# Gathers in buffers of two groups, layer 2 one step later, transposes moved up, and last node parts placed by hand in a graph layer

## The chip, the core and the metric

One Trainium2 chip, one core of it. The metric is the device time of one execution in microseconds (us); it is the median of three runs. The profile is of one further execution of the same program on the chip.

## What is computed

A message-passing layer on 12,500 nodes with 64 features and 200,000 edges sorted by target, then a residual and a layer norm. In short:

```python
nodes = x[edges].reshape(E, 128)                     # x[src] beside x[dst], gathered per edge
gates = ssp(edge_attr @ We1 + be1) @ We2 + be2       # ssp(v) = softplus(v) - log 2
gates = gates * (1 - sigmoid(5 * (dist - 3.5)))
h     = ssp(nodes @ Wn1 + bn1) @ Wn2 + bn2
msum  = zeros_like(x).at[dst].add(h * gates)         # sums over the edges of each target node
y     = x + (x + (ssp(msum @ Ws1 + bs1) @ Ws2 + bs2))
out   = (y - mean(y)) / sqrt(var(y) + 1e-5)
```

All of it is in float32.

## The kernel before, in words

**Groups and steps.** The edges go in NG = 391 groups of 512 (two halves of 256, four chunks of 128 lanes, K = 4). The main loop runs over steps `i` from -3 to 388; in one step different groups are in different stages, so a step has the work of one group altogether. The order on each engine is the order in which the code calls things (`tc.manual_schedule()`); waits between engines are put in by the framework.

**The start.** The part of `x[dst] @ Wn1` is first made once per node as a table in DRAM ("the table phase", L497 to L519): 14 pieces, each of 7 matmuls (L501), a copy by ACT (L503), one by DVE (L504), a store, and a memset of the buffer that becomes `sums` (L506).

**Gathers.** `gather(g)` (L173) fetches `x[src]` for a group: four indirect DMAs issued by POOL (L183), one per chunk, into an `xg` buffer. 12 groups out of 391 (`by_rows`) have three, and their last chunk comes by single rows on SP's queue (`fetch`, L198). There are AHEAD + 5 = 25 `xg` buffers, one per group. Six groups are gathered at once, one more after each of the 14 table pieces (its gather waits for a one-column memset on DVE, L178, which stands behind that piece), and in step `i` the group `i + 19`. A gather into a used buffer waits for the last reader of the group that had it, 25 groups earlier: the scatter matmul of L292.

**One step `i`, before.** On PE: `layer2_edge(i-1)` (L266 bias, L269); `layer1_edge(i+1)` (L233 bias, L235) into a new `z` tile (two of them, in PSUM); node-block matmuls, if any are due; `layer1_node(i+1)` (L241); `scatter(i-3)` (L292) into the free end of the same `z` tile; `transposes(i+3)` (L224) into a `tx` tile (two); `layer2_node(i-1)` (L275) into the `gh` tile (two). On ACT: `exps` and `logs` of group `i+1` (L252, L255), then `xcopy(i+3)` (L229, `tx` to SBUF). On DVE: `hcut` and `message` of `i-1` (L284, L288), `window(i-3)` (L308, adds the scatter's result to `sums`), `softplus(i+1)` (L260), `onehot(i+5)` (L216). SP loads edge features and table rows some steps ahead (L204, L211).

`second`, `third` and `ahead` say which groups are in layer 2, scatter and transposes in a step. Near the end (from `ends = last - CATCH_UP` = 373) the order in a step changes and the lags shrink, so that the last groups are not strung out.

**Node blocks.** 25 blocks of up to 512 nodes are finished as soon as all their edges are summed: `node_block` returns 11 parts (fetch, hidden L327, logs, center, ssp, layer2 L358, add, square, variance, root, scale and store), which `BLOCK_STEPS` spreads over the steps that follow. The last block is done after the loop (L620 to L647).

Of the kernel before, what the change touches and what calls it, by code (L numbers as in the profile page):

```python
# [42 lines left out]
F32 = mybir.dt.float32  # L43
# [13 lines left out]
P = 128  # L57
D = 64
HE = 256
GE = 2 * HE  # L60
W = 42
# [1 line left out]
PIECES = 3  # L63
NB = 512
K = 4
AHEAD = 20
LOADS = 5
SPREADS = 5
CATCH_UP = 17
PREPARE = 5  # L70

BLOCK_STEPS = ((2, 3, 4, 4, 6, 7, 8, 9, 10, 14), (2, 3, 3, 4, 5, 6, 7, 8, 9, 10), (1, 1, 1, 2, 3, 3, 4, 4, 4, 4))
ROWS = 4
CUTOFF = 5.0
EPS = 1e-5
# [28 lines left out]
def gnn_resnorm_kernel(ctx: ExitStack, tc: tile.TileContext, a: dict, out: bass.AP, E: int):  # L104
# [67 lines left out]

    def gather(g, after=False):  # L173

        xg = loads.tile([P, K, P], F32, name="xg", bufs=AHEAD + 5)
        xgs[g] = xg
        if after:
            nc.vector.memset(xg[:, 0, :1], 0.0)  # L178
        for k in range(K - (g in by_rows)):
            if padding(g, k):  # L180
                nc.vector.memset(xg[:, k, :D], 0.0)
                continue
            nc.gpsimd.indirect_dma_start(  # L183
                out=xg[:, k, :D], out_offset=None, in_=x,
                in_offset=bass.IndirectOffsetOnAxis(ap=src_i[:, g, k : k + 1], axis=0))
# [70 lines left out]

    def softplus(g, part=every):
        if part.start == 0:
            ss[g] = work.tile([P, 3, 2, P], F32, name="s", bufs=3)
        nc.vector.scalar_tensor_tensor(ss[g].rearrange("p i t e -> p (i t e)")[:, part], us[g][:, part], BIG,  # L260
                                       z_of(g)[:, part], OP.min, OP.max)

    def layer2_edge(g):
        gh = gh_tile()
        v = gh.rearrange("p (i t h d) -> p i t h d", i=2, t=2, h=2)
        nc.tensor.matmul(gh, ones3[:, :P], row3.rearrange("q i k d -> q (i k d)"), start=True, stop=False,  # L266
                         skip_group_check=True)
        for t in range(2):
            nc.tensor.matmul(v[:, 0, t], ss[g][:, 0, t, :], we2, start=False, stop=False, skip_group_check=True)  # L269
        ghs[g] = gh.rearrange("p (i k d) -> p i k d", i=2, k=K)  # L270
# [127 lines left out]
    with tc.manual_schedule():  # L398
# [4 lines left out]
        with tc.tile_pool(name="prep", bufs=1) as prep:  # L403
# [15 lines left out]
            nc.sync.dma_start(dist, a["dist_l"])  # L419
            dst_i = rel.bitcast(I32)  # L420
            nc.sync.dma_start(dst_i.rearrange("p g k -> p (g k)"), a["dst_l"])
            FREE = AHEAD - 2 * PARTS
            for g in range(FREE):
                gather(g)

            nc.vector.memset(one, 1.0)
            nc.vector.memset(half, 0.5)
# [68 lines left out]
            for i in range(PARTS):  # L496
                for c in range(i * CP, (i + 1) * CP, CP // 2):  # L497
                    m = CP // 2
                    ps = z_tile().rearrange("p b (k f) -> p (b k) f", k=K)
                    for k in range(m):  # L500
                        nc.tensor.matmul(ps[:, k, :], xT[:, c + k, :], wnb, start=True, stop=True)  # L501
                    tb = prep.tile([P, m, 2 * D], F32, name="tb", bufs=6)
                    nc.scalar.copy(tb[:, :K, :], ps[:, :K, :])  # L503
                    nc.vector.tensor_copy(tb[:, K:, :], ps[:, K:m, :])  # L504
                    nc.sync.dma_start(by_node[:, c : c + m], tb)
                    nc.vector.memset(sums[:, c * P : WIDE if c + m == NCH else (c + m) * P], 0.0)  # L506
                    gather(FREE + c // m, after=True)
                if i == 1:
                    nc.vector.tensor_copy(base_i, base_b[:1])
                    for k in range(2):  # L510
                        nc.vector.tensor_copy(be3[:, k, :], rows[:, 0, :])
                    for k in range(K):
                        nc.vector.tensor_copy(row3[:, :, k, :], rows[:, 1:3, :])
                        nc.vector.tensor_copy(rs3[:, k, :], rows[:, 3, :])
                if i == 2:
                    nc.vector.tensor_copy(rel, dst_i)
                    for t in range(2):
                        r = rel[:, :, 2 * t : 2 * t + 2]
                        nc.vector.tensor_sub(r, r, base_b[:, :NH].rearrange("p (g h) -> p g h", h=2))  # L519


        with tc.tile_pool(name="finish", bufs=1) as finish:
# [5 lines left out]
            def lagging(i, lag, steps):  # L528

                lag -= sum(i > step for step in steps)  # L530
                return [g for g in range(i - lag, i - lag + 1 + (i in steps)) if g >= 0]

            for i in range(-3, NG):
                second[i] = lagging(i, 1, (ends + 5,))
                third[i] = lagging(i, 3, (ends - 2, ends + 8))
                ahead[i] = [i + 3] if i < ends else [i + 2] if i == ends + 1 else [i + 1] if i > ends + 2 else []
            parts, begun, complete = {}, None, 0

            def at(f, g, *more):
                if 0 <= g < NG:  # L540
                    f(g, *more)
# [5 lines left out]
            for i in range(-3, last - 1):  # L547
# [1 line left out]
                early = [part for part in now if part.tensor]  # L549
                at(load, i + LOADS)  # L550
                fetch(i)
                if i > 0:
                    at(gather, i + AHEAD - 1)
                if i < ends:
                    for g in second[i]:
                        layer2_edge(g)
                    if i >= -1:
                        zs[i + 1] = z_tile()
                        layer1_edge(i + 1)
                        for part in early:  # L560
                            part.tensor(tx_tile())
                    if i >= -1:
                        layer1_node(i + 1)
                    for n, g in enumerate(third[i]):
                        scatter(g, zs[i + 1][:, 1, HE + 2 * W * n : HE + 2 * W * (n + 1)])
                    at(exps, i + 1)
                    at(logs, i + 1)
                    for g in ahead[i]:
                        transposes(g)
                        xcopy(g)  # L570
                    for g in second[i]:
                        layer2_node(g)
                    for g in second[i]:
                        hcut(g)
                        message(g)
# [34 lines left out]
                    begun.pop(0).others()  # L610
                if blocks and complete >= blocks[0][1]:
                    steps = next(steps for steps in BLOCK_STEPS if i + steps[-1] < last - 1)
                    for n, part in zip(steps, begun, strict=True):
                        parts.setdefault(i + n, []).append(part)
                    blocks.pop(0)
                    begun = None
            assert len(blocks) == 1 and begun and not parts
# [8 lines left out]
            for some in (edge, node):  # L626
                exps(last, some)
                logs(last, some)
            for g in range(last - 2, last + 1):
                window_bases(g)  # L630
            layer2(last - 1)
# [5 lines left out]
            scatter(last - 1, tx_tile()[:, : 2 * W])  # L637
            softplus(last, node)
            window(last - 2)
            layer2_node(last)  # L640
            window(last - 1)
            hcut(last)
            message(last)
            scatter(last, tx_tile()[:, : 2 * W])
            window(last)
            for part in begun:
                node_part(part)  # L647

# [146 lines left out]
```

## Time and profile before

| what | value |
|---|---|
| median of three runs (2535.73 to 2542.47) | 2539.01 us |
| the profiled execution, own time | 2535.25 us |
| its span, first to last instruction | 2533.4 us |
| granted TensorE clock, mean | 0.866 |
| busy: PE, PE weight loads | 2139.0 us, 1735.4 us |
| busy: POOL, DVE, ACT | 1469.2 us, 1085.8 us, 920.1 us |
| gathers on POOL (L183) | 1551, 0.947 us each |
| exponentials (L252) | 392, 0.809 us each |

How to read it: busy times are of one engine each, and engines work beside each other, so they don't add up. "Idle before, released by" in a timeline row names whose signal came last by the profile before an instruction could start. PE's rows are pipelined, and their ends are modelled. A timeline row has the start in us from the span's start, the duration in us, the engine, the source line, the operation, the output tile with the input tiles, and in brackets the idle time before it.

### The profile page before, as it was taken

What the parts mean: (1) busy time and instruction counts of PE and PEld (TensorE: products, weight loads), DVE (VectorE), ACT (ScalarE), POOL (GpSimd) and SP (SyncE); (2) the same over time, 40 slices, a digit from 0 to 9 for tenths busy, and PEclk for the clock granted to TensorE, in tenths of its full rate; (3) what the DMA queues carried; (4) which work ended last, traced back from release to release, by engine and by line L of the source; (5) the groups of instructions that cost most, each with busy time, mean ns of one, the idle gap of its engine ahead of it and who ended that gap; (6) DMA issues with size and microseconds to landing.
All of it is one profiled execution on the core that took longest, in us unless ns stands there. A gap on an engine that the chain in (4) does not pass through costs nothing. (4 is left out here: it accounts for less than half of the span.)

```text
span 2533.4 us, 41076 instructions
## 1 busy us (share of the span) xinstructions
PE 2139.0 (84%) x11373; PEld 1735.4 (69%) x11373; DVE 1085.8 (43%) x2745; ACT 920.1 (36%) x1317; POOL 1469.2 (58%) x1555
## 2 busy tenths in 40 slices
PE   4569888988988888888879987988898889888897
PEld 3457676777767767667767766766777667766775
DVE  3224434444444444444444444444444444444553
ACT  1123333333333333333333433333434333333442
POOL 6655666666666666656666655566666666666400
PEclk9998889788888888888997888888888888899895
DMA  7312222222222222222222222222222222222210
GB/s 194 90 45 52 51 50 53 51 51 53 51 55 50 53 52 55 53 52 57 51 55 56 50 53 53 52 57 52 57 54 53 56 54 57 55 61 55 54 48 8
DMA packets 170982, 143.07 MB, mean 56 GB/s; under 512 B 46475, under 2 KB 142915, under 8 KB 170746
## 3 DMA queue, kind: packets, MB, share of 16 engines
q1 hardware_dynamic: 119746, 87.95, 12.0%
q0 software_dynamic: 49632, 50.92, 11.2%
q8 instruction: 93, 1.52, 0.3%
q10 hardware_dynamic: 1368, 1.51, 0.2%
q14 instruction: 143, 1.17, 0.1%
HBM read 130.57 MB, written 9.63 MB: 55 GB/s over the span
## 5 line engine op out<-in xcount | busy, mean ns | idle before, releaser
L183 POOL DMA_INDIRECT xg<-in_x,src_i x1551 | 1469.0, 947 | 919.4 <-issue 361.1
L252 ACT ACTIVATE u<-z 128x768 f32<-128x768 f32 x392 | 317.0, 809 | 1435.7 <-PE z L241 469.1
L284 DVE TENSOR_TENSOR h<-gh,cut 128x256 f32<-128x256 f32 x391 | 165.9, 424 | 1162.9 <-PE z L241 369.9
L241 PE MATMUL z<-xT,wns 106*128 106x256 f32 x1564 | 497.2, 448 | 7.1 <-issue 3.2
L275 PE MATMUL gh<-consts,s 128*128 128x64 f32 x3128 | 428.9, 284 | 7.0 <-issue 6.9
L269 PE MATMUL gh<-consts,s 128*128 128x128 f32 x1564 | 310.5, 326 | 141.7 <-issue 124.1
L275 PEld LDWEIGHTS gh<-consts,s 128*128 128x128 f32 x3128 | 423.6, 210 | 4.8 <-issue 4.8
L241 PEld LDWEIGHTS z<-xT,wns 106*128 106x128 f32 x1564 | 353.1, 228 | 78.7 <-issue 8.5
L269 PEld LDWEIGHTS gh<-consts,s 128*128 128x128 f32 x1564 | 229.0, 211 | 248.7 <-issue 222.7
L260 DVE SCALAR_TENSOR_TENSOR s<-u,z 128x768 f32<-128x768 f32 x392 | 372.7, 951 | 47.6 <-issue 26.2
L255 ACT ACTIVATE u<-u,one 128x768 f32<-128x768 f32 x392 | 365.9, 933 | 12.7
L224 PE MATMUL tx<-consts,xg 128*106 128x128 f32 x1552 | 278.4, 307 | 62.8 <-ACT u L255 29.4
L235 PE MATMUL z<-eT,consts 128*128 128x256 f32 x782 | 314.7, 489 | 0.0
L292 PEld LDWEIGHTS z<-xg,msg 128*128 128x128 f32 x1484 | 272.0, 227 | 47.5 <-issue 16.1
L292 PE MATMUL z<-xg,msg 128*128 128x84 f32 x1484 | 257.0, 298 | 21.1 <-issue 20.7
L224 PEld LDWEIGHTS tx<-consts,xg 128*106 128x106 f32 x1552 | 209.9, 160 | 86.6 <-issue 38.2
L229 ACT COPY xT<-tx 106x512 f32<-106x512 f32 x391 | 221.4, 566 | 35.9 <-PE tx L224 18.5
L308 DVE TENSOR_TENSOR sums<-sums,z 64x42 f32 x742 | 145.8, 197 | 129.1 <-issue 113.9
L288 DVE TENSOR_TENSOR msg<-gh,h 128x256 f32<-128x256 f32 x391 | 165.9, 424 | 13.4
L235 PEld LDWEIGHTS z<-eT,consts 128*128 128x128 f32 x782 | 131.9, 212 | 54.9 <-issue 16.1
L266 PE MATMUL gh<-row,ones 3*128 3x512 bf16 x391 | 156.9, 401 | 3.3 <-issue 2.5
L216 DVE TENSOR_TENSOR xg<-consts,rel 128x168 f32<-128x168 f32 x391 | 135.9, 348 | 0.2
(100 smaller groups left out, 635.7 us busy)
## 6 DMA issues: line engine op xcount, KB each, us to landing
eT<-in_eT SPq DMA_DIRECT2D x391, 128.0 KB
xg<-in_x,src_i POOLq DMA_INDIRECT x1551
xr<-in_x SPq DMA_DIRECT2D x1536, 0.2 KB
wns<-table SPq DMA_DIRECT2D x782, 21.0 KB
table<-tb SPq DMA_DIRECT2D x14, 448.0 KB
sums<-in_xT SPq DMA_DIRECT2D x7, 455.0 KB
y<-in_x SPq DMA_DIRECT2D x24, 128.0 KB
out<-y SPq DMA_DIRECT2D x24, 128.0 KB
```

What stands on the lines that cost most here:

```text
L183: nc.gpsimd.indirect_dma_start(out=xg[:, k, :D], out_offset=None, in_=x, in_offset=bass.IndirectOffsetOnAxis(ap=src_i[:, g, k : k + 1], ax ...
L224: nc.tensor.transpose(tx[:, k, :], row, ident)
L229: nc.scalar.copy(xT, xTs[g])
L235: nc.tensor.matmul(zs[g][:, 0, :HE], we1.rearrange("a h d -> a (h d)"), eTs[g], start=False, stop=True, skip_group_check=True)
L241: nc.tensor.matmul(zn, wns[:, g % REST, h, :], xTs[g][:, h], start=True, stop=True, skip_group_check=True)
L252: nc.scalar.activation(us[g][:, part], z_of(g)[:, part], AF.Exp)
L255: nc.scalar.activation(us[g][:, part], us[g][:, part], AF.Ln, bias=one)
L260: nc.vector.scalar_tensor_tensor(ss[g].rearrange("p i t e -> p (i t e)")[:, part], us[g][:, part], BIG, z_of(g)[:, part], OP.min, OP.max)
L269: nc.tensor.matmul(v[:, 0, t], ss[g][:, 0, t, :], we2, start=False, stop=False, skip_group_check=True)
L275: nc.tensor.matmul(ghs[g][:, 1, 2 * t + h, :], ss[g][:, 1 + h, t, :], wn2, start=False, stop=h == 1 and t == 1, skip_group_check=True)
L284: nc.vector.tensor_mul(hs[g], ghs[g][:, 1], cut[:, g, :].to_broadcast([P, K, D]))
L292: nc.tensor.matmul(sc, msgs[g][:, 2 * t : 2 * t + 2, :].rearrange("p h f -> p (h f)"), xgs[g][:, 2 * t : 2 * t + 2, D:DW], start=t == 0, s ...
```

## The change

- `xg` buffers hold two groups: one buffer `[P, 2, K, P]` for groups `2p` and `2p+1`, (AHEAD + BEHIND) // 2 = 11 of them, that is 22 groups in place of 25.
- Gathers of two groups are issued in every second step (`i` and even): groups `i + 16` and `i + 17`, the first with the DVE memset while `i < 6`.
- In the table phase seven groups are gathered at once and nine more at pieces 0, 1, 3, 5, 6, 8, 10, 11 and 13, so 16 groups and not 20.
- Layer 2 stands two steps behind (`i-2`), the scatter four (`i-4`); there are four `s` buffers in place of three. On PE a step is now: layer 2 (edge and node together), transposes, layer 1 edge, scatter, layer 1 node.
- The end begins 10 groups before the last and not 17, with new steps at which the lags shrink; the parts of the last but one block from the square on, and the last block's first, are placed by hand after the loop.

```diff
-AHEAD = 20
+AHEAD = 16
-CATCH_UP = 17
+CATCH_UP = 10
+FREE = 7
+BEHIND = 6
-BLOCK_STEPS = ((2, 3, 4, 4, 6, 7, 8, 9, 10, 14), (2, 3, 3, 4, 5, 6, 7, 8, 9, 10), (1, 1, 1, 2, 3, 3, 4, 4, 4, 4))
+BLOCK_STEPS = ((2, 3, 4, 4, 6, 7, 8, 9, 10, 14), (2, 3, 3, 4, 5, 6, 7, 8, 9, 10), (1, 2, 1, 2, 3))
...
     def gather(g, after=False):
-        xg = loads.tile([P, K, P], F32, name="xg", bufs=AHEAD + 5)
-        xgs[g] = xg
+        if g % 2 == 0:
+            pair = loads.tile([P, 2, K, P], F32, name="xg", bufs=(AHEAD + BEHIND) // 2)
+            xgs[g], xgs[g + 1] = pair[:, 0], pair[:, 1]
+        xg = xgs[g]
...
-            ss[g] = work.tile([P, 3, 2, P], F32, name="s", bufs=3)
+            ss[g] = work.tile([P, 3, 2, P], F32, name="s", bufs=4)
...
-            FREE = AHEAD - 2 * PARTS
-            for g in range(FREE):
-                gather(g)
+            waiting = {}
+            for g in range(AHEAD):
+                if g < FREE:
+                    gather(g)
+                else:
+                    waiting.setdefault(min(5 * (g - FREE) // 3, 2 * PARTS - 1), []).append(g)
...
-                    gather(FREE + c // m, after=True)
+                    for g in waiting.get(c // m, []):
+                        gather(g, after=True)
...
-                second[i] = lagging(i, 1, (ends + 5,))
-                third[i] = lagging(i, 3, (ends - 2, ends + 8))
+                second[i] = lagging(i, 2, (ends - 3, ends + 3))
+                third[i] = lagging(i, 4, (ends - 4, ends - 2, ends + 5))
...
-                if i > 0:
-                    at(gather, i + AHEAD - 1)
+                if i >= 0 and i % 2 == 0:
+                    at(gather, i + AHEAD, i < BEHIND)
+                    at(gather, i + AHEAD + 1)
                 if i < ends:
                     for g in second[i]:
-                        layer2_edge(g)
+                        layer2(g)
+                    for g in ahead[i]:
+                        transposes(g)
+                        xcopy(g)
                     if i >= -1:
                         zs[i + 1] = z_tile()
                         layer1_edge(i + 1)
                         for part in early:
                             part.tensor(tx_tile())
+                    for n, g in enumerate(third[i]):
+                        scatter(g, zs[i + 1][:, 1, HE + 2 * W * n : HE + 2 * W * (n + 1)])
                     if i >= -1:
                         layer1_node(i + 1)
-                    for n, g in enumerate(third[i]):
-                        scatter(g, zs[i + 1][:, 1, HE + 2 * W * n : HE + 2 * W * (n + 1)])
                     at(exps, i + 1)
                     at(logs, i + 1)
-                    for g in ahead[i]:
-                        transposes(g)
-                        xcopy(g)
-                    for g in second[i]:
-                        layer2_node(g)
...
-                    for n, part in zip(steps, begun, strict=True):
+                    for n, part in zip(steps, begun):
                         parts.setdefault(i + n, []).append(part)
+                    rest = begun[len(steps) :]
...
+            square, variance, root, scale, store = (part.others for part in rest)
+            square()
...
             window(last - 2)
+            variance()
+            root()
             layer2_node(last)
...
             window(last)
+            hidden, clamp = begun.pop(0)
+            hidden(gh_tile())
+            scale()
+            clamp()
+            store()
```

## The prediction

> **What bounds the kernel now.** I read the page first (PE 84% busy, POOL 58%, ACT 36%, DVE 43%: no engine is full), then the table of waits (ACT's L252, DVE's L284 and POOL's L183 all wait for PE, in turn for many different PE lines), then the timeline of all engines in an undisturbed stretch:
>
> ```profile
> 1202.15 0.94 POOL L183 DMA_INDIRECT xg<-in_x,src_i  x1 [1.46 <-PE tx L224]
> ...
> 1206.47 0.39 PE L266 MATMUL gh<-row,ones 3*128 3x512 bf16 x1
> 1206.53 0.81 ACT L252 ACTIVATE u<-z 128x768 f32<-128x768 f32 x1 [1.51 <-PE gh L275]
> ...
> 1206.76 0.42 DVE L284 TENSOR_TENSOR h<-gh,cut 128x256 f32<-128x256 f32 x1 [1.70 <-PE gh L275]
> 1206.77 0.94 POOL L183 DMA_INDIRECT xg<-in_x,src_i  x1 [1.18 <-PE gh L275]
> ...
> 1210.51 1.06 POOL L183 DMA_INDIRECT xg<-in_x,src_i  x1 [0.30 <-issue]
> 1210.82 0.39 PE L266 MATMUL gh<-row,ones 3*128 3x512 bf16 x1
> ...
> 1212.61 0.81 ACT L252 ACTIVATE u<-z 128x768 f32<-128x768 f32 x1 [3.83 <-PE z L233]
> ...
> 1212.84 0.42 DVE L284 TENSOR_TENSOR h<-gh,cut 128x256 f32<-128x256 f32 x1 [2.09 <-PE z L235]
> 1212.85 0.94 POOL L183 DMA_INDIRECT xg<-in_x,src_i  x1 [1.28 <-PE z L235]
> ```
>
> See that ACT, DVE and POOL, which wait for three different matmuls (L241, L275, L292), wake within 0.24 us of each other, 2.1 to 2.3 us after the last of a group's gathers was issued (1210.51). PE's own records come 4.35 us apart (1206.47 to 1210.82); the wakes are 6.08 us apart. The step that begins at 1202.15 has three gathers (its fourth chunk is one of the 12 by single rows) and lasts 4.62 us. So a step is as long as its gathers: while they run, news that PE has finished something is held back. POOL waits each step because its buffer is freed by PE's scatter, so the loop is POOL, PE's news, POOL. Over the trace I counted 340 cycles of four gathers, median 6.06 us.
>
> Two other places bear this out: a run of eight gathers (POOL), and, after the last gather (2387.93), ACT's rows of L252, which are then 4.5 us apart:
>
> ```profile
> 345.48 0.94 POOL L183 DMA_INDIRECT xg<-in_x,src_i  x1 [2.82 <-PE z L241]
> ...
> 354.22 0.94 POOL L183 DMA_INDIRECT xg<-in_x,src_i  x1 [0.30 <-issue]
> 357.21 0.95 POOL L183 DMA_INDIRECT xg<-in_x,src_i  x1 [2.04 <-PE z L292]
> ```
>
> ```profile
> 2427.21 0.81 ACT L252 ACTIVATE u<-z 128x768 f32<-128x768 f32 x1 [1.22 <-PE z L241]
> 2431.72 0.81 ACT L252 ACTIVATE u<-z 128x768 f32<-128x768 f32 x1 [1.22 <-PE z L241]
> ```
>
> The start shows the same on a larger scale: 32 gathers in a row (105.22 to 143.90) leave ACT waiting from 118.5 to 144.05 for all but a copy, and POOL resumes at 161.93:
>
> ```profile
> 116.67 0.81 ACT L252 ACTIVATE u<-z 128x768 f32<-128x768 f32 x1 [3.96 <-PE z L233]
> 144.05 0.81 ACT L252 ACTIVATE u<-z 128x768 f32<-128x768 f32 x1 [18.32 <-remote]
> ```
>
> **Budget of before**, from POOL's rows. POOL's first loop wait (group 25) ends at 161.93; its last (group 390) at 2385.43, 365 cycles later. 365 x 6.06 = 2211.9; the 12 short ones take 6.06 - 4.62 = 1.44 less each, 17.3; the remaining 2385.43 - 161.93 - 2211.9 + 17.3 = 28.9 is cycles lengthened by node blocks. From 2385.43 to the end are 148.0. Sum 2533.4, the span.
>
> **The change, part by part.**
>
> *The loop.* A gather of an even group now waits once for DVE's memset or for the scatter of a group 11 pairs earlier, and eight gathers (seven with a short group) follow without a wait: 365 cycles become 184 (first pairs waited for: 22/23; last 390). What does one cost? By the run of eight, 357.21 - 345.48 = 11.73; the other clean ones in the trace took 11.90, 12.14 and 12.22. Against 2 x 6.06 = 12.12, the lower end is what saving one of two restarts gives (four more gathers cost 11.73 - 6.06 = 5.67, 1.42 each). I take 11.85: the two low ones are nearer, because the high ones start amid node-block work. PE has 2 x 4.35 = 8.70 to do in it, and about 0.44 of node blocks (0.74 for L358 and the like, in some steps), so spare 2.7. 184 x 11.85 = 2180.4.
>
> For this to hold, PE must do two groups with the news of one wake. That is where the lag of two goes: layer 2 of group i-2 and i-1 can follow from softplus results that DVE made after one wake, and `z`, `gh` and `tx` have two buffers each, so PE can go two steps beyond what was reported. The exponential of the second step waits for its layer 1 as before; its news comes with the next wake.
>
> *The other moves of the order cost nothing while that holds:* the scatter stood between L241 and L252's release only in the free end of `z` (0.57 us, inside the held time); `xcopy` (0.56) now goes ahead of the exponential on ACT, inside ACT's 3.8-us idle time before L252 (1212.61); without that cover it is 0.56 a step. `onehot` of an even group now waits for eight gathers, but they were issued 11 steps earlier. SP's queue keeps its order: loads, fetches and table rows move past nothing. The counts of PE, ACT and DVE instructions stay; a fourth `s` buffer only takes a wait away. The memset is 0.06 us, in three steps only.
>
> *The start.* The table phase now stands behind 64 gathers and not 68 (17 groups were gathered by 105.22). 3.4 + 64 x 1.42 = 94.3, and some 3 us of gaps: the last piece at 97 where before it was about 107; 9.6 us on (softplus of group 0, as in before, 109.75 to 119.4) the first pair of the loop may go. Three pairs (groups 16 to 21) each follow a softplus: 11.73 + 2.82 (the wait of 345.48's row) = 14.5 each, so POOL's first wait for a scatter ends at 106.6 + 43.5 = 150. Bounds: 106.6 + 3 x 11.73 = 142, and 162 as before.
>
> *The end.* Group 390's gather now waits for the scatter of 369, in step 373; 16 steps and what is behind the last exponential remain (in before 2509.1 to 2533.4, 24.3). At 4.5 a step that is 97. In before, the exponential of step 373 (2409.05) stood 124.3 before the end, as the clock was 0.50 from 2478 on. I take 110: the shorter catch-up leaves less half-filled work, but the same dependent end. The hand-placed parts of block 24 (square to store) lie beside PE's L327 and L275 of the last groups; without cover the scale's four operations of 0.163 and the store's issue cost 1.1.
>
> **Sum:** 150 + 2180.4 - 17.3 + 28.9 + 110 = 2452.0, that is 81.4 less than the span of 2533.4. The profiled execution (2535.25) lies 3.8 below the median 2539.01, and its span 1.9 below its own time; I take the 81.4 from the median: 2457.6, so **2458 us**.
>
> **Two rules weighed.** The clock, by windows of before (us, then busy time and count of PE, PEld, DVE, ACT, POOL, then granted clock, DMA share, GB/s):
>
> ```profile
> 1180.00:1200.00 20.00, 17.84 (x70) 14.60 (x71) 7.26 (x20) 6.65 (x9) 12.38 (x14) 0.66 0.22 49
> 1200.00:1220.00 20.00, 19.40 (x124) 15.87 (x122) 10.81 (x26) 8.68 (x13) 12.12 (x13) 1.00 0.22 49
> ```
>
> Both stretches have the same steps per gather, at clocks of 0.66 and 1.00: the clock doesn't set the step now. In finer windows the half clock comes in pieces of 3.4 us, each of which costs PE 1.7 us of work; one in each cycle of 11.85 fits into the spare 2.7, two (3.4) don't. The Trainium skill ("TensorE: Matmul & The Clock Gate", "Why this matters for your kernels") speaks against longer cycles: it wants no idle gaps of PE over about 3 us, and says that one such window halves the clock; a cycle with one wake gives just such a gap. By it every cycle would have at least one slow window, which the sum allows for. The second rule: the skill's "DMA: Bandwidth & Descriptors", in "Anatomy of one DMA — SWDGE (gpsimd) path", puts the making of descriptors down as small; by it, leaving out one gather should not shorten a step, and pairing them would bring nothing in the loop, which gives about 2508. The three-gather step, 1.44 us shorter with the same PE work, disagrees.
>
> **The rivals.** *A, only the ends gain.* A cycle of eight costs two of four, 12.12, because each chunk holds news as long as before and PE's restart merely moves. For it: 12.14 and 12.22 among the clean runs. Against it: 11.73 and 11.90. 184 x 0.27 = 49.7 more: 2507. *B, slower: PE doesn't get through two groups in one hold.* After a wake it must wait for exponential, logarithm and softplus (0.81 + 0.94 + 0.95 = 2.7 us), so it idles near 3 us, the clock falls, and two half-clock pieces come in each cycle: 8.70 + 0.44 + 3.4 = 12.54, 0.69 above mine, 184 x 0.69 = 127: 2585. It decides from 12.29 on, where 184 x 0.44 has eaten the 81.4. For it: the clock of 0.66 above, and one run of eight that took 18.07, with a node block in it. Against: four that took no more than 12.22, without any lag made for them. *C, it doesn't do what it says:* POOL finds the next pair's buffer free already and runs 16 or more in a row, as at the start. The one run of 12 in the trace took 17.73, 1.48 a gather, so eight would again cost 11.8; with no restart at all 8 x 1.434 = 11.47 and 2388. Against it: the pair's scatter is reported only by a wake.
>
> **How the numbers follow.** Forecast 0.60, A 0.20, B 0.15, C 0.05. My own case by its corners: 142 + 184 x 11.73 + 11.6 + 97 = 2409 span, 2415 at the median's level; 162 + 184 x 12.22 + 11.6 + 124 = 2546, 2552; corners seldom meet, so 2410 to 2505 for the forecast alone. With A inside, and part of B and C: 2400 to 2535. Some 0.3% (7.6 us) is what a measurement here can tell from no change: faster 0.80, same 0.05 (from B's lower edge), slower 0.15.
>
> **What would show it.** Right: POOL's waits before L183 every 11.7 to 11.9 us with eight issues between; its first scatter wait ending near 150 and its last 2342 or so; PE with one idle stretch near 3 us a cycle; a mean clock at or below 0.87; 110 us behind the last wake. Wrong: wakes in the middle of a run of eight (then the news isn't held by gathers); cycles over 12.3 with PE busy right up to the wake (B); runs of 16 (C); cycles of 12.1 (A); or ACT idle before L252 gone, with `xcopy` in the chain.

## The result, and the profile after

The changed kernel takes **2855.34 us** (median of four runs, 2849.59 to 2858.87) against 2540.74 us for the kernel before on the same chip: **1.124 times as long** (95% interval 1.1204 to 1.1267). The forecast was 2458, with 2400 to 2535 as its range. What happened is nearest to rival B, which had a chance of 0.15 and a time of 2585.

The page of the changed kernel, its first lines and the row of the granted clock in 40 slices, and behind them the same row of the kernel before:

```profile
span 2855.7 us, 40645 instructions
...
PE 2602.5 (91%) x11373; PEld 1959.3 (69%) x11373; DVE 1052.5 (37%) x2743; ACT 936.5 (33%) x1317; POOL 1468.8 (51%) x1555
...
PEclk9776666776676865677868568576676677666687
```

```profile
PEclk9998889788888888888997888888888888899895
```

The same 11,373 matmuls now take 463 us more of PE, and the clock row, nearly all 8 and 9 before, is mostly 6 and 7. The mean granted clock is 0.706 (0.866 before). PE is busier only because it is slower.

By the budget of the prediction, from POOL's rows: the first scatter wait ends at 144.87 (150 forecast), the last at 2741.08, and 114.6 us follow (110 forecast). Start and end are right within 5 us or so each. The whole miss is the loop: 2596.2 us for 184 cycles, **14.11 us a cycle** where 11.85 (with the node blocks 11.91) was forecast.

The 173 cycles of exactly eight gathers are of two kinds. 72 take 12.35 us or less: 71 of them 12.22 on average, at a mean clock of 0.92. The others take up to 25 us, most of them at a clock of 0.5 to 0.7; 32 of them 16.34, at 0.51. Two windows of the changed kernel show both kinds (span, busy time and count of PE, PEld, DVE, ACT, POOL, granted clock, DMA share, GB/s), first two clean cycles, then one slow one:

```profile
2211.45:2235.95 24.50, 21.60 (x117) 16.61 (x116) 10.81 (x28) 9.60 (x15) 15.20 (x16) 0.86 0.21 49
1208.65:1224.90 16.25, 16.25 (x58) 12.32 (x58) 8.56 (x22) 6.14 (x9) 7.55 (x8) 0.50 0.18 40
```

In the slow one PE is busy for all of the 16.25 us: the 58 matmuls of two steps, at half clock. The timeline of that slow cycle has POOL's last gather, the bias matmul of layer 2 (L271, once a step), and POOL's next start:

```profile
1217.39 0.94 POOL L188 DMA_INDIRECT xg<-in_x,src_i  x1 [0.31 <-issue]
1218.17 0.60 PE L271 MATMUL gh<-row,ones 3*128 3x512 bf16 x1
...
1224.90 0.94 POOL L188 DMA_INDIRECT xg<-in_x,src_i  x1 [6.57 <-PE z L297]
...
1226.34 0.60 PE L271 MATMUL gh<-row,ones 3*128 3x512 bf16 x1
```

A step is 8.17 us (1218.17 to 1226.34) where it was 4.35 at full clock, and POOL waits 6.57 us for a scatter that PE reaches late. The gathers are no longer the bound in such a cycle. PE is.

A clean cycle of the changed kernel isn't as forecast either. Its second half:

```profile
2231.75 0.24 PE L297 MATMUL z<-xg,msg 128*128 128x84 f32 x1
2232.32 0.23 PE L297 MATMUL z<-xg,msg 128*128 128x84 f32 x1 [0.34 <-issue]
2232.40 0.94 POOL L188 DMA_INDIRECT xg<-in_x,src_i  x1 [0.31 <-issue]
2233.73 0.19 PEld L297 LDWEIGHTS z<-xg,msg 128*128 128x128 f32 x1 [1.79 <-issue]
...
2234.42 0.23 PE L297 MATMUL z<-xg,msg 128*128 128x84 f32 x1 [1.87 <-issue]
...
2235.15 0.23 PE L297 MATMUL z<-xg,msg 128*128 128x84 f32 x1 [0.49 <-issue]
...
2235.31 0.81 ACT L257 ACTIVATE u<-z 128x768 f32<-128x768 f32 x1 [4.57 <-remote]
2235.95 0.94 POOL L188 DMA_INDIRECT xg<-in_x,src_i  x1 [2.61 <-PE z L246]
```

The four matmuls of one scatter (0.57 us when undisturbed) take from 2231.75 to 2235.38, with waits that the profile puts down to nothing ("issue"); no instruction of the scatter waits for a semaphore in the program. PE comes to a stop of its own, some 1.75 steps after the last wake, and goes on as the eight gathers end. The scatter that POOL waits for stands behind that stop, so POOL starts 3.55 us after its last issue (2232.40), where the run of eight that the forecast used took 2.99 (354.22 to 357.21). That is where 12.2 us come from. The kernel before has such stops at its scatter too (us in total, times, longest), all but one of them at instructions that wait for no semaphore:

```profile
PE z L292 <- issue: 20.7, 45, 1.1
```

### The profile page after: what moved, and what is told of

Same layout as the page of the kernel before. It is cut to its first block, busy times and chain, and to the rows that moved or that the text cites. A ratio compares the mean times of both kernels' runs of the same rounds, so it can differ in the third digit from the quotient of the medians.

```text
span 2855.7 us, 40645 instructions
## 1 busy us (share of the span) xinstructions
PE 2602.5 (91%) x11373; PEld 1959.3 (69%) x11373; DVE 1052.5 (37%) x2743; ACT 936.5 (33%) x1317; POOL 1468.8 (51%) x1555
## 5 line engine op out<-in xcount | busy, mean ns | idle before, releaser
L246 PE MATMUL z<-xT,wns 106*128 106x256 f32 x1564 | 620.0, 530 | 49.8 <-issue 45.4
L280 PE MATMUL gh<-consts,s 128*128 128x64 f32 x3128 | 540.6, 334 | 3.1 <-issue 3.1
L280 PEld LDWEIGHTS gh<-consts,s 128*128 128x128 f32 x3128 | 537.1, 258 | 3.2 <-issue 3.2
L297 PEld LDWEIGHTS z<-xg,msg 128*128 128x128 f32 x1512 | 325.2, 264 | 96.9 <-issue 56.1
L240 PE MATMUL z<-eT,consts 128*128 128x256 f32 x782 | 374.5, 571 | 3.7 <-issue 3.6
L274 PE MATMUL gh<-consts,s 128*128 128x128 f32 x1564 | 369.2, 372 | 4.4 <-issue 4.3
L274 PEld LDWEIGHTS gh<-consts,s 128*128 128x128 f32 x1564 | 275.2, 248 | 131.5 <-issue 130.8
L297 PE MATMUL z<-xg,msg 128*128 128x84 f32 x1512 | 309.2, 334 | 60.2 <-issue 59.8
L229 PE MATMUL tx<-consts,xg 128*106 128x128 f32 x1552 | 323.4, 347 | 26.1 <-issue 13.4
L229 PEld LDWEIGHTS tx<-consts,xg 128*106 128x106 f32 x1552 | 250.3, 190 | 31.9 <-issue 15.4
L271 PE MATMUL gh<-row,ones 3*128 3x512 bf16 x391 | 187.9, 481 | 1.9 <-PE z L246 1.3
L271 PEld LDWEIGHTS <-ones 3*128 3x128 bf16 x391 | 36.8, 94 | 197.3 <-issue 179.9
```

Source lines behind the costliest of these rows:

```text
L229: nc.tensor.transpose(tx[:, k, :], row, ident)
L240: nc.tensor.matmul(zs[g][:, 0, :HE], we1.rearrange("a h d -> a (h d)"), eTs[g], start=False, stop=True, skip_group_check=True)
L246: nc.tensor.matmul(zn, wns[:, g % REST, h, :], xTs[g][:, h], start=True, stop=True, skip_group_check=True)
L280: nc.tensor.matmul(ghs[g][:, 1, 2 * t + h, :], ss[g][:, 1 + h, t, :], wn2, start=False, stop=h == 1 and t == 1, skip_group_check=True)
L297: nc.tensor.matmul(sc, msgs[g][:, 2 * t : 2 * t + 2, :].rearrange("p h f -> p (h f)"), xgs[g][:, 2 * t : 2 * t + 2, D:DW], start=t == 0, s ...
```

## The experiments

The chips differ, which was not known beforehand. On the chip of the result (its number isn't known, and it may be one of the two) and on chips 5 and 7, the kernel before takes 2515 to 2543 us and gathers hold PE's news back as the prediction read it. On chips 1, 4, 6, 11 and 12 the kernel before takes 2008 to 2022 us and nothing is held back. Why they differ isn't shown; chips 1 and 12 were met twice each and were of the second kind both times. Thirteen of the eighteen runs came to the second kind. Each run below is compared with the kernel before on its own chip.

### On chip 5, where gathers hold the news (kernel before 2542.99 us)

**e1_pairs_alone**: the kernel before with only the gathers paired.

```diff
-        xg = loads.tile([P, K, P], F32, name="xg", bufs=AHEAD + 5)
-        xgs[g] = xg
+        if g % 2 == 0:
+            pair = loads.tile([P, 2, K, P], F32, name="xg", bufs=13)
+            xgs[g], xgs[g + 1] = pair[:, 0], pair[:, 1]
+        xg = xgs[g]
...
-                if i > 0:
-                    at(gather, i + AHEAD - 1)
+                if i >= 0 and i % 2 == 0:
+                    at(gather, i + AHEAD)
+                    at(gather, i + AHEAD + 1)
```

> The kernel before with only the gathers changed: buffers of two groups (13 of them), eight gathers in every second step; order, lags and ends as before. Theory 'order' (the slow cycles come from the new order of PE's step, in which the half clock is rarely left): clean cycles of about 12.2 us, mean clock about 0.87, time 2500 to 2570. Theory 'pairs' (eight gathers in a row stop PE for some 3 us, and the half clock that follows makes any order bound by PE at 8.17 us a step): mean cycle 13.5 to 14.5, clock near 0.70, time 2750 or more.

Measured: 2862.9 us, ratio 1.127 (1.1213 to 1.1328), clock 0.803. As slow as the whole change, without its order and lags. The time is as theory 'pairs' had it, the clock is not (near 0.70 expected).

**e2_singles**: the changed kernel with one group per buffer and four gathers in every step.

```diff
-        if g % 2 == 0:
-            pair = loads.tile([P, 2, K, P], F32, name="xg", bufs=(AHEAD + BEHIND) // 2)
-            xgs[g], xgs[g + 1] = pair[:, 0], pair[:, 1]
-        xg = xgs[g]
+        xg = loads.tile([P, K, P], F32, name="xg", bufs=AHEAD + BEHIND)
+        xgs[g] = xg
...
-                if i >= 0 and i % 2 == 0:
-                    at(gather, i + AHEAD, i < BEHIND)
-                    at(gather, i + AHEAD + 1)
+                if i >= 0:
+                    at(gather, i + AHEAD, i < BEHIND and i % 2 == 0)
```

> The changed kernel with one group per buffer (22) and four gathers in every step; order, lags and ends as changed. Theory 'pairs': cycles of 6.07 us, mean clock 0.86, time 2500 to 2560. Theory 'order': half-clock stretches stay long (mean over 12 us against 7.3 in the kernel before), clock below 0.80, time 2600 to 2850.

Measured: 2660.72 us, ratio 1.0475 (1.0381 to 1.0568), clock 0.772. Order, lags and ends (with 22 buffers for 25) cost 4.75% by themselves; time, clock and stretches are as theory 'order' had them. In the loop the half clock lasts 28 us at a time (6.8 in the kernel before).

**e3_old_order**: the changed kernel with the old order of a step.

```diff
                     for g in second[i]:
-                        layer2(g)
-                    for g in ahead[i]:
-                        transposes(g)
-                        xcopy(g)
+                        layer2_edge(g)
                     if i >= -1:
                         zs[i + 1] = z_tile()
                         layer1_edge(i + 1)
...
+                        layer1_node(i + 1)
                     for n, g in enumerate(third[i]):
                         scatter(g, zs[i + 1][:, 1, HE + 2 * W * n : HE + 2 * W * (n + 1)])
-                    if i >= -1:
-                        layer1_node(i + 1)
                     at(exps, i + 1)
                     at(logs, i + 1)
+                    for g in ahead[i]:
+                        transposes(g)
+                        xcopy(g)
+                    for g in second[i]:
+                        layer2_node(g)
```

> The changed kernel with the order of a step on PE and ACT as before (layer 2 edge, layer 1 edge, layer 1 node, scatter, transposes, layer 2 node), while pairs, lags of two and four and ends stay as changed. Theory 'order': half-clock stretches fall to about 7 us, cycles of eight gathers to 12.2 us, time 2480 to 2560. Theory 'pairs': time 2750 or more, clock about 0.70.

Measured: 2807.42 us, ratio 1.1052 (1.0955 to 1.1149), clock 0.79. The half-clock stretches fall to 10.9 us, but the time hardly falls. Theory 'pairs' had this time, but not the clock (0.70) nor the way, half clock that makes PE the bound in any order; the pairs lose it otherwise. Over the loop (170 us to 120 us before the end), from the records of clock and matmuls (before and changed on the chip of the result, the others on chip 5):

| kernel | span | half clock, us | stretches, mean us | PE stopped, us | of it in stops over 3 us |
|---|---|---|---|---|---|
| before | 2533 | 621 | 91, 6.8 | 292 | 58 in 14 |
| changed | 2856 | 1583 | 67, 23.6 | 180 | 37 in 5 |
| e2, order without pairs | 2651 | 1177 | 42, 28.0 | 157 | 0 |
| e1, pairs without order | 2860 | 1044 | 105, 9.9 | 447 | 172 in 23 |
| e3, pairs, lags, old order | 2814 | 1116 | 102, 10.9 | 401 | 155 in 22 |

(The expectations give stretches of 7.3 us for the kernel before, which is the mean over its whole trace, and of 18 us for the changed kernel, where the same count gives 24.)

With pairs under the old order PE stops more often. The first three rows of the table of waits of PE (us in total, times, longest) in e3 are:

```profile
PE tx L229 <- issue: 113.2, 102, 10.4
PE tx L229 <- DMA xr<-in_x: 58.9, 6, 11.4
PE tx L332 <- DVE sums L313: 47.6, 11, 6.3
```

The first is put down to nothing. In the second the single rows that SP fetches for the short groups come late (7.0 us in the kernel before, 63.8 in e1), and SP's queue holds loads whose buffers PE must free, news of which now comes half as often. I did not try whether that is the reason.

Why half clock costs time even in shorter stretches can be read from e1's cycles of eight, sorted by their clock. The 77 at a clock of 0.85 or more take 12.32 us on average, and PE is stopped for 2.27 of them; the 48 at 0.70 to 0.85 take 13.78, and PE is stopped for 2.15. PE is busy 1.58 us longer in these, and its stop is hardly shorter: by this count the slower work did not go into the time of the stop.

**e4_three**: the kernel before with the fourth chunk of each group set to zero and not gathered.

```diff
-            if padding(g, k):
+            if padding(g, k) or k == K - 1:
                 nc.vector.memset(xg[:, k, :D], 0.0)
                 continue
```

> The kernel before, with three gathers per group: the fourth chunk of each group is set to zero by VectorE and not gathered (the output is not the reference's). If gathers hold back PE's news, a step falls from 6.06 to about 4.6 to 4.8 us and the time to 1980 to 2100, at a clock of 0.95 or more. If PE's own work or the clock sets the step of 6.06, the time stays above 2450.

Measured: 2176.11 us, ratio 0.8567 (0.8522 to 0.8611), clock 0.917; the median cycle of three gathers is 4.66 us. POOL's rows that follow a wait:

```profile
1200.14 1.11 POOL L183 DMA_INDIRECT xg<-in_x,src_i  x1 [1.75 <-PE z L292]
...
1204.95 0.95 POOL L183 DMA_INDIRECT xg<-in_x,src_i  x1 [1.20 <-PE tx L224]
...
1209.54 0.94 POOL L183 DMA_INDIRECT xg<-in_x,src_i  x1 [1.14 <-DVE l_s L350]
```

4.81 and 4.59 us apart with the same work on PE. One gather less is 1.4 us less: on such a chip gathers set the step, as the prediction said. The time missed the expected 2100 by 76 us, as some cycles were longer (mean 5.23), and the clock stayed under the expected 0.95.

### What the traces say of the clock

The granted clock changes on a grid of 3.413 us in all these traces. I sorted the windows at half clock of the six kernels so far (before, changed, e1 to e4) by what PE did in them, and asked whether the next window had full clock:

| in the window | full clock next |
|---|---|
| PE stopped for over 4% of it | 9 of 335 |
| PE busy, with more than some 0.12 us of one of the two 3-row bias matmuls (layer 1 edge, layer 2 edge) | 53 of 919 |
| PE busy, less or nothing of a bias matmul | 375 of 447 |

With any part of a bias matmul, however short, it is 105 of 999, and 323 of 370 without: the cut at 0.12 us doesn't make the difference.

In the old order, at half clock, layer 1's bias matmul starts 1.69 us after layer 2's, and the next of layer 2 comes 6.41 us later; less its own 0.39, 6.0 us are free of both, and many windows fit in. In the new order layer 2's node part and the transposes stand between them: 4.14 us from one to the other and 4.03 back, less 0.60 and 0.39, leave two free pieces of 3.5 and 3.6 us, into which a window of 3.4 rarely fits: some 365 of the changed kernel's 463 half-clock windows hold a bias matmul. That was a reading only; the next kernels try it.

**e5_wide** (the operands of the bias matmuls padded from 3 rows to 128, one of the two with zeros, so that the sums stay), **e6_bias_moved** (layer 1's bias matmul issued right behind layer 2's), and **e7_before_b2** (the kernel before, with layer 2's bias matmul issued a step earlier, between scatter and transposes):

```diff
# e5_wide
-    ones3 = const.tile([PIECES, HE], BF16, name="ones3")
-    be3 = const.tile([PIECES, 2, D], BF16, name="be3")
-    row3 = const.tile([PIECES, 2, K, D], BF16, name="row3")
+    ones3 = const.tile([P, HE], BF16, name="ones3")
+    be3 = const.tile([P, 2, D], BF16, name="be3")
+    row3 = const.tile([P, 2, K, D], BF16, name="row3")
...
+            nc.vector.memset(be3, 0.0)
+            nc.vector.memset(row3, 0.0)
...
# e6_bias_moved, in layer2_edge behind its bias matmul
+        if with_bias is not None:
+            layer1_bias(with_bias)
...
# e7_before_b2, between scatter and transposes
+                    if i + 1 < ends and second[i]:
+                        layer2_bias(i)
```

> The changed kernel, with the two bias matmuls of a step made from 128 rows (125 of them zero) in place of 3; same results, same instructions. In all runs so far a 3.4-us window at half clock with no bias matmul in it led back to full clock in 375 of 447 cases, one with a bias matmul in 53 of 919. Theory 'three rows' (the monitor counts rows in use, so a 3-row matmul looks idle): half-clock stretches fall from 18 us to 4 to 7 us, mean clock to 0.85 or more, cycle to about 12.5, time to 2500 to 2600. Theory 'bubble' (it is the weight load or the change of type around them that counts, not the rows): no change, 2840 to 2870, clock 0.70.

> The changed kernel, with one instruction a step moved: the bias matmul of layer 1 follows directly on that of layer 2, so that some 7 us (at half clock) of a step are free of bias matmuls in one piece, in place of two pieces of 4 us. If windows without bias matmuls bring the clock back: half-clock stretches of about 7 us in place of 18, time 2550 to 2680. If the pairs alone make the time: 2820 or more.

> The kernel before, with one instruction a step moved: the bias matmul of layer 2 is issued one step earlier, between the scatter and the transposes, so that it and the one of layer 1 stand some 4 us apart (at half clock) on both sides. Gathers one group a step, as before. If the place of the bias matmuls sets how long the half clock lasts: half-clock stretches of 12 to 28 us in place of 7.3, mean clock 0.75 to 0.80, time 2600 to 2700. If not: 2530 to 2550.

Measured on chip 12, where the kernel before takes 2022.03 us: e5 1992.44, ratio 0.9873 (0.9774 to 0.9972); e6 1998.1, 0.9876 (0.9864 to 0.9888); e7 2019.58, 1.0005 (0.9973 to 1.0037). They tell nothing of the time that half clock costs, as the clock hardly falls there (0.982, 0.972, 0.956), but show the other kind of chip. The timeline of e7, where L299 is the scatter and stands before L252 as in the kernel before:

```profile
1000.66 0.57 PE L299 MATMUL z<-xg,msg 128*128 128x84 f32 x4
1000.91 0.94 POOL L183 DMA_INDIRECT xg<-in_x,src_i  x1 [0.30 <-PE z L241]
...
1001.27 0.81 ACT L252 ACTIVATE u<-z 128x768 f32<-128x768 f32 x1 [2.10 <-PE z L299]
...
1002.16 0.94 POOL L183 DMA_INDIRECT xg<-in_x,src_i  x1 [0.30 <-issue]
```

ACT starts 0.04 us after the scatter's end, in the middle of the gathers. POOL issues one every 1.25 us without a wait (four are 5.0 us a step), and that is the bound there: 1552 x 1.25 = 1940.

**e8_after** and repeats. The same three kernels and the changed kernel itself were run again together:

> The changed kernel itself, beside the three above on their chip. Where gathers hold the news: 2855 as before. Where they do not: both kernels are bound by the issue of the gathers, 1552 x 1.25 = 1940 us plus some 45 at the end, so 1985 to 2010 against 2022, the same within 2%.

> The changed kernel with 128-row bias matmuls again (the chip of the last runs let PE's news through while gathers ran: the kernel before took 2022 there, so nothing was told of the half clock). Where gathers hold the news (kernel before near 2540): theory 'three rows' 2500 to 2600 with half-clock stretches of 4 to 7 us; theory 'bubble' 2840 to 2870. Where they do not (before near 2022): 1990 again.

> The changed kernel with layer 1's bias matmul next to layer 2's, again. Where gathers hold the news: 2550 to 2680 with half-clock stretches of about 7 us if windows without bias matmuls bring the clock back, 2820 or more if not. Where they do not: 1998 again.

> The kernel before with layer 2's bias matmul moved away from layer 1's, again. Where gathers hold the news: 2600 to 2700 with half-clock stretches of 12 to 28 us if the place of the bias matmuls sets how long the half clock lasts, 2530 to 2550 if not. Where they do not: 2020 again.

They came to chip 1 (kernel before 2017.32). The changed kernel: 1993.98 us, ratio **0.9876** (0.9825 to 0.9926); e8_wide 0.9908 (0.9863 to 0.9952); e8_bias_moved 0.988 (0.9822 to 0.9938); e8_before_b2 1.0017 (0.9992 to 1.0042). So on a chip that lets the news through the change gains 1.2%, and neither edit of the bias matmuls adds to it. Once more for two of them:

> The changed kernel with 128-row bias matmuls, for a chip on which gathers hold the news (kernel before near 2540). Theory 'three rows': half-clock stretches 4 to 7 us in place of 18, time 2500 to 2600. Theory 'bubble': 2840 to 2870. On a chip that lets the news through (before near 2020): about 1995, and nothing is told.

> The kernel before with layer 2's bias matmul moved 4 us away from layer 1's, for a chip on which gathers hold the news. If the place of the bias matmuls sets how long the half clock lasts: stretches of 12 to 28 us in place of 7.3, time 2600 to 2700; if not, 2530 to 2550. On a chip that lets the news through: about 2020, and nothing is told.

Chip 1 again: 0.9881 (0.9838 to 0.9923) and 1.0003 (0.9971 to 1.0035), as before.

Though the times tell nothing of it, the traces of these runs show what brings the clock back, in kernels without any stop made by hand. For windows at half clock with PE busy and any part of a bias matmul, and for the stretches over the loop (their number and mean length):

| kernels | full clock next | half-clock stretches, us |
|---|---|---|
| changed (e8_after) | 1 of 12 | 2, 23.9 |
| changed, 128 rows (e5, e8, e9) | 25 of 25 | 26, 5.7 |
| changed, bias moved (e6, e8) | 0 of 14 (without a bias matmul 21 of 23) | 22, 7.6 |
| before, layer 2's bias moved (e7, e8, e9) | 22 of 104 | 31, 12.8 |

The last had a mean clock of 0.953 over its 24 runs, the kernel before beside it 0.967 over 33. So the rows and places of the bias matmuls act on the clock as the reading has it; that costs no time there, where POOL is the bound.

**s1_segments**: four variants in stretches of the loop of one kernel, so that one run could tell. The steps from 285 also have a small matmul ahead of the transposes that takes their waits.

```diff
+    def rows_of(step):
+        return slice(0, P if step // PART in (1, 3) else PIECES)
...
+                    moved = i // PART == 2
...
+    def first_look(g):
+        looked[g] = tx_tile()
+        n = K - (g in by_rows)
+        nc.tensor.matmul(looked[g][:, :n], ident, xgs[g][:, :n, 0], start=True, stop=True, skip_group_check=True)
```

> The changed kernel in four stretches of its loop: steps 0 to 94 as it is; 95 to 189 with the bias matmuls made from 128 rows (125 zero); 190 to 284 with 3 rows but layer 1's bias matmul moved next to layer 2's; from 285 with 128 rows, and with one small matmul a step ahead of the transposes that takes their waits for the gathers, so that PE signals 8 times a step and not 10. On a chip where gathers hold the news (kernel before near 2540), by cycle of eight gathers: theory 'three rows' 14.1 us in the first stretch, 12.2 to 12.6 in the second, about 13 in the third, and in the fourth 12.2 to 12.6, or 11.7 to 11.9 if PE stops for too many signals not yet delivered. Theory 'pairs alone': 14 in all four. On a chip that lets the news through (before near 2020): near 10.0 in all four.

It came to chip 4: 2002.76 us beside 2019.22. So did its repeats s3, s4 and s5 (chips 6, 11 and 12), with 2019.16 beside 2015.95, 1996.03 beside 2007.59, and 1996.96 beside 2017.51. Each of these times is one run.

> The same kernel as in s1_segments, for a chip on which gathers hold the news (kernel before near 2540): by pair of steps, 14.1 us as changed (steps 0 to 94); with 128-row bias matmuls 12.2 to 12.8 and half-clock stretches near 6 us (95 to 189); with layer 1's bias matmul moved next to layer 2's 12.2 to 13.0, stretches near 5 us (190 to 284); from 285, 128 rows and eight signals a step in place of ten: as the second stretch, or 11.7 to 11.9 if PE stops because too many of its signals wait for delivery. If the half clock is not what costs the time, 14 in all four.

> Once more the kernel of s1_segments, for a chip on which gathers hold the news (before near 2540): by pair of steps 14.1 us in steps 0 to 94; 12.2 to 12.8 with 128-row bias matmuls (95 to 189); 12.2 to 13.0 with the bias matmul moved (190 to 284); from 285 as the second stretch, or 11.7 to 11.9 if the number of PE's signals is what stops it. 14 in all four if the half clock is not what costs the time.

> The kernel of s1_segments a last time, for a chip on which gathers hold the news (before near 2540): by pair of steps 14.1 us in steps 0 to 94; 12.2 to 12.8 with 128-row bias matmuls (95 to 189); 12.2 to 13.0 with the bias matmul moved (190 to 284); from 285 as the second stretch, or 11.7 to 11.9 if the number of PE's signals is what stops it. 14 in all four if the half clock is not what costs the time.

On these chips POOL's issue sets the pace, so the times of the stretches tell nothing. Whether fewer signals of PE would shorten the clean cycle of 12.2 us stays untried.

**s2_paused**: to stop PE on any chip, a small matmul in every second step waits for the exponential, the logarithm and one copy of the group just done; the four stretches differ in the bias matmuls and in the order.

```diff
+    def pause(g):
+        stall = work.tile([P, 3 * HE], F32, name="stall", bufs=1)
+        nc.scalar.copy(stall, us[g])
+        nc.tensor.matmul(zs[g][:, 1, NB - 4 :], ident, stall[:, :4], start=True, stop=True, skip_group_check=True)
...
+    def rows_of(step):
+        return slice(0, P if step // PART == 1 else PIECES)
...
                     at(exps, i + 1)
                     at(logs, i + 1)
+                    if i > 0 and i % 2 == 1:
+                        pause(i + 1)
```

> The changed kernel with a pause of PE made by hand in every second step (a small matmul after layer 1 waits for ScalarE's exponential, logarithm and one more copy, about 3 us), so that PE stops once in eight gathers on any chip; in four stretches of the loop: steps 0 to 94 order as changed, 3-row bias matmuls; 95 to 189 the same with 128 rows; 190 to 284 3 rows, layer 1's bias matmul moved next to layer 2's; from 285 3 rows and the order of the kernel before. Full clock would give 2 x 4.35 + 3 = 11.7 us a pair of steps, half clock throughout 16.3 + 3. Theory 'three rows': first stretch 13.5 to 16 us with half-clock stretches over 10 us; second 11.7 to 12.7 with stretches of 3.4 to 7; third and fourth between, 12.3 to 13.5. Theory 'bubble' or dtype: the second like the first. Theory 'the pause alone': all four alike.

It came to chip 7, which holds the news (kernel before 2515.01 in one run): 3185.82 us. Windows over the four stretches of s2_paused, columns as before:

```profile
186.80:964.20 777.40, 662.78 (x2416) 504.26 (x2416) 205.11 (x512) 229.82 (x296) 315.58 (x332) 0.57 0.13 34
995.70:1613.80 618.10, 481.72 (x2655) 427.10 (x2653) 231.65 (x593) 245.87 (x339) 338.13 (x358) 0.79 0.18 47
1641.70:2277.40 635.70, 498.01 (x2711) 408.39 (x2711) 243.59 (x631) 249.69 (x352) 345.63 (x365) 0.83 0.19 48
2306.10:2995.10 689.00, 572.28 (x2541) 462.54 (x2539) 238.75 (x616) 241.47 (x340) 317.23 (x334) 0.73 0.16 42
```

The clock rises from 0.57 to 0.79 when the rows are 128 and nothing else in the code differs. By stretch:

| stretch | us a pair of steps | half clock, mean stretch us | windows with a bias matmul that led to full clock |
|---|---|---|---|
| new order, 3 rows | 18.73 | 29.0 | 1 of 125 |
| new order, 128 rows | 13.58 | 6.3 | 42 of 43 |
| new order, 3 rows, bias moved | 13.97 | 4.6 | 0 of 3 |
| old order, 3 rows | 16.21 | 9.4 | 12 of 67 |

Theory "three rows" holds in what it says of the clock: the same instructions, with 125 rows of zeros added, turn a window that hardly ever brought the clock back into one that does, and moving one 3-row matmul does nearly as much (46 of the third stretch's 49 windows with PE busy hold no bias matmul, and all 46 led to full clock). Whether the rows of the matmul or of its weight load count can't be told, as both were padded. The sizes were missed: all four stretches took longer than their ranges, by 2.7, 0.9, 0.5 and 2.7 us a pair. In the first PE was busy for 16.0 us a pair, near the 16.3 of half clock throughout, and stopped for 2.7. In the second it was busy for 10.6, where the work at full clock is 8.7 (some 9.1 with node blocks), and stopped for 3.0: 263 of its 618 us still ran at half clock.

## Why the prediction was wrong

- **What bounds the kernel before** was read rightly: gathers hold back PE's news. e4_three, with one gather less, took 4.66 us a step where 4.62 was read. But that holds on some chips only, which one trace can't show.
- **Start and end** came within 5 us or so of their terms; the node blocks' 28.9 can't be told apart in the loop. In the start that is partly luck: the sum has three pairs with a wait of 2.82 each, but in the trace two pairs went as 16 gathers without a wait (from 104.83, as rival C feared for the loop) and the third then waited 8.50 for DVE's memset.
- **"I take 11.85"** was too short. Clean cycles take 12.22. 184 x 0.37 = 68 us of the loss; rival A had 12.12. The step under it that failed is "PE can go two steps beyond what was reported": PE stops some 1.75 steps beyond, in a scatter that waits for nothing, and POOL waits for that scatter. Two buffers of every PSUM tile don't help there, since the stop is not a wait for one. The sign of it was in the trace of before: the 45 stops at L292. The trace's records of PE's semaphore show some 13 updates undelivered at the stop, of ten a step; that their number is what stops PE is argued, not shown.
- **"One in each cycle of 11.85 fits into the spare 2.7"** is the step that cost most. It took half clock to last one piece of 3.4 us a cycle. In the kernel before that was so for 31 of 93 stretches (mean 7.3 us over the whole trace), and it was carried over to another order, in which stretches last 23.6 us on average (67 of them). A cycle inside one is bound by PE at 2 x 8.17 = 16.34. The 336 us of the loss that the clean cycles don't explain (2596.2 - 2192.0 - 68) lie nearly all in these slow cycles. With the old order the spare 2.7 didn't take the half clock up either: in e1's cycles PE is stopped for over 2 us at any clock. Rival B had the right place, but the same size: two pieces of 3.4 a cycle, 12.54 instead of 14.11.
- **"The clock doesn't set the step now"** rests on two windows said to have the same steps per gather. POOL's cycles are alike in them, but PE has 70 matmuls beside 14 gathers at 0.66 and 124 beside 13 at 1.00, some 2.4 and 4.3 steps of 29. PE fell behind at half clock and made up for it later. That the pairs leave no room for this is likely, but not shown.
- **"The other moves of the order cost nothing while that holds"** is false. The new order and lags, with single groups, cost 4.75% (e2_singles). I counted what each instruction costs and what covers it, and not how the new order spaces the two 3-row bias matmuls.
- The **rule on the clock** that spoke against the change pointed the right way. The Trainium skill, "TensorE: Matmul & The Clock Gate", "What's actually happening", says that one busy window of about 3.4 us brings the full clock back. The measurement differs here: of 919 half-clock windows in which PE was busy but a 3-row matmul ran, 53 led to full clock.
- The **pairs alone** (e1_pairs_alone, 1.127) are as slow as the whole change, and order and lags alone cost over a third of that, so the two don't add up: without the long half clock the pairs would lose 10.5% all the same (e3_old_order, 1.1052). With the old order the pairs lose by stops of PE (447 us against 292) and half clock that returns oftener (105 stretches); with the new order by half clock that stays. That the spacing of the bias matmuls makes it stay is shown by s2_paused and by the traces on chips 1 and 12; that PE stops more often with pairs is measured, and why is open. What the changed kernel would take with 128-row bias matmuls on a chip of the first kind stays open: it ran on the second kind only.

## What to carry to other kernels

Before moving matmuls, find in the trace what brings the clock back after a stop, and how long a stretch of such work the order leaves; 3-row matmuls like these should stand together or be padded with zero rows, which cost no time in s2_paused (layer 2's took 381 ns with 128 rows and 385 with 3, at full clock). A wait taken away by doing two turns at once can make the rest wait twice as long for news, so every chain of hand-overs (node blocks, single-row fetches) has to be costed at the new interval. And a gain or loss that rests on contention should be measured on more than one chip: this change is 12% slower on one and 1.2% faster on another.

## What the hardware showed that was not expected

- Chips of one kind differ: the kernel before takes 2515 to 2543 us on chips 5 and 7 and on that of the result, and 2008 to 2022 us on five others; on the latter PE's news passes while gathers run (ACT 0.04 us behind the scatter).
- With news held back PE itself stops, in instructions that wait for no semaphore, with gaps of 1.8 us between the matmuls of one scatter.
- For the clock a 3-row matmul works like idle time and a 128-row one with 125 zero rows like work: 1 of 125 windows against 42 of 43 led back to full clock, and 1 of 12 against 25 of 25 in the changed kernel without a pause.
